# Self-attention on one Trainium2 core: the inputs' rounding moved behind a maximum of scores, the variances of the heads placed behind it, and the keys' part of the rounded inputs written first

## The chip, the cores and the metric

The kernel runs on one core of one Trainium2 chip. A core has a matrix engine (TensorE, PE in the profile, with PEld for its weight loads), a vector engine (VectorE, DVE), a scalar engine (ScalarE, ACT), a general engine (GpSimd, POOL) and an engine that only issues transfers (SyncE, SP). Each runs its own instructions strictly in order and waits on semaphores for the others. The metric is the device time of one execution in microseconds; the kernel before took 1504.7 us (median of 3 runs, 1503.29 to 1509.96).

## What is computed

The input x is 16 sequences of 128 tokens of width 256. Four blocks follow each other, each added to x: a gated attention with keys and values from x itself ("self", 16 heads in 8 groups of width 128) and from a context ("cross", 16 more heads), a feed-forward block, a causal attention with 32 small heads, and a mixture of 8 experts. The change touches the first:

```python
ln_out = _ln(hidden_states, ln_w, ln_b)
q = _ln(_fp8_linear_pertensor(ln_out, wq, wq_scale, q_in_scale).reshape(...), qln_w, qln_b)
k = _ln(_fp8_linear_pertensor(ln_out, wk, ...), kln_w, kln_b)      # each head normalised
v = _fp8_linear_pertensor(ln_out, wv, ...)
core = _gqa(q, k, v)                                               # softmax attention
qx = _ln(_fp8_linear_pertensor(ln_out, wqx, ..., qx_in_scale), ...) # queries of the cross part
...
catq = _div_clamp_fp8(cat, proj_smooth)                            # both parts, rounded
return einsum(catq, wproj) * (proj_in_scale * proj_w_scale)
```

`_fp8_linear_pertensor` divides its input by a scale per channel, clamps it to 448, rounds it to bfloat16 and then to an 8-bit float, and multiplies it by the weights. So one layer-normed x is rounded four times, for q, k, v and qx.

## The kernel before

**Units and steps.** A unit is one sequence's self or cross attention: units 0 to 15 are self, 16 to 31 cross. A unit has 16 heads in four chunks of four heads, and a loop over n (L692) makes one step per chunk: step n holds the scores of chunk n, and, shifted by fixed numbers of steps, everything else. `do(n, lag, name)` calls a stage for the chunk `lag` steps back (ahead where it is negative), `once(n, step, name)` calls a stage once per unit, at the unit's first step plus `step`. So the steps of one unit run mixed with the projections of the next and the preparation of the one after it.

**What sets the order.** The program is written in the order of these calls. A scheduler then orders each engine's instructions by its own estimate of what is ready, with the written order as priority, and puts in the semaphores; what the engines run is therefore near the written order but not equal to it. `stay_after(ins, other)` (L102) tells the scheduler that one instruction must stand behind another of the same engine, without a semaphore.

**A self unit's preparation.** `prep_norm`, `prep_tr` and `prep_scale` make the normalised x, transposed and divided by the four scales: one tile in_y of 128x1024 (four kinds of 2x128 columns, in the order q, k, v, qx), scaled on GpSimd (L387). `prep_round` (L397) rounds it with the helper `e4m3` (L219): four instructions on VectorE (L225 clamp, L226 exponent, L230, L231), each needing the one before, and a subtraction on GpSimd (L237) that `prep_last` issues one step later. It writes xs (q, k and v, 128x768) and xx (qx, 128x256); xx also goes to DRAM by the SyncE queue (L409), for the cross unit of the same sequence. The same helper, with the same lines, rounds the attention's output (`quant`, tile cat_y, 128x1024, twice a unit).

**Projections and heads.** `project` multiplies xs by the weights (L431; keys first, then queries, then values, two blocks of 512 columns a step), `evict` copies the result from PSUM on ScalarE (L443 raw for keys and queries, L440 vt for values), `bn` takes each head's statistics on VectorE (L452). `rstd` (L454) makes the 24 heads' variances of a unit (L459 q_dif, L460, L461, L464 q_var) and their inverse roots (`rsqrt0`: L308 and L309 on ScalarE, then L310 to L312 on VectorE, the last writing q_r). `mult` scales raw by q_r on GpSimd (L475), `heads` transposes it on TensorE (L486) and copies it on ScalarE into kT and qT (L495).

**Attention.** `scores` (L504), `top` (L512, the negated maximum on VectorE), `exp` (L520, four instructions on ScalarE with their sums), `recip` (L528) and `divide` (L532, GpSimd), `probs` (L540 transposes, L542 copy), `values` (L550), `smooth` (L561, VectorE, writes cat_y), `quant`, `quant_last` (L237, GpSimd, writes cat), `output` (L591).

**Where the change works.** In the third of every four steps (n = 4u + 2), the step in which the unit's third chunk has its scores, `prep_last` of the unit after next, and `rstd` of the next unit, fall together. In the kernel before, `prep_round` closes the step before that one (`once(n, -7, "prep_round")`, L735), and in the step itself the calls are: scores, probs, top, exp, a projection, `prep_last` (L710), values, smooth, bn, `rstd` (L715), then mult and heads.

Of the kernel before, what the change touches and what calls it, by code (L numbers as in the profile page):

```python
# [35 lines left out]
def flamingo_kernel(  # L36
# [182 lines left out]
    def e4m3(dsts, y, pool):  # L219


        n = y.shape[1]
        e = pool.tile([P, n], BF16, tag="e8_e", name="e8_e")
        t = pool.tile([P, n], BF16, tag="e8_t", name="e8_t")
        nc.vector.tensor_scalar(y, y, FP8_MAX, -FP8_MAX, ALU.min, ALU.max)  # L225
        nc.vector.tensor_scalar(  # L226
            e.bitcast(U16), y.bitcast(U16), 0x7F80, None, ALU.bitwise_and
        )

        nc.vector.tensor_scalar(e, e, 2.0**-6, 24.0, ALU.max, ALU.mult)  # L230
        nc.vector.tensor_tensor(t, y, e, ALU.add)  # L231

        def last(other=None):
            at = 0
            for dst in dsts:
                part = slice(at, at + dst.shape[1])
                ins = nc.gpsimd.tensor_tensor(dst, t[:, part], e[:, part], ALU.subtract)  # L237
                if other is not None:
                    stay_after(ins, other)
                at += dst.shape[1]  # L240

        return last
# [11 lines left out]
    with (  # L254
# [59 lines left out]

        norms = {}
# [19 lines left out]
        class Unit:  # L335
# [61 lines left out]
            def prep_round(self):  # L397
                if self.cross:
                    return
                xs = ap.tile([P, 6 * P], F32R, tag="xs", name="xs")  # L400
                xx = ap.tile([P, KD * P], F32R, tag="xx", name="xx")
                self.last = e4m3([xs, xx], self.y.rearrange("p i t -> p (i t)"), ap)
                self.xs, self.xx = xs, xx

            def prep_last(self):
                if self.cross:
                    return
                self.last()
                nc.sync.dma_start(out=xqx[self.b], in_=self.xx.bitcast(F32))  # L409
                lhs = [  # L410
                    [self.xs[:, (2 * kind + k) * P : (2 * kind + k + 1) * P] for k in range(KD)]
                    for kind in range(3)
                ]
                self.q_lhs, self.k_lhs, self.v_lhs = lhs[K_Q], lhs[K_K], lhs[K_V]
# [39 lines left out]
            def rstd(self):  # L454
# [4 lines left out]
                nc.vector.tensor_tensor(dif, st[:, :, 1], st[:, :, 4], ALU.subtract)  # L459
# [4 lines left out]
                nc.vector.scalar_tensor_tensor(var, var, 1.0 / P, dif, ALU.mult, ALU.add)  # L464
# [45 lines left out]
            def top(self, c):  # L510
                mx = small.tile([P, 4], F32, tag="mx", name="mx")
                nc.vector.tensor_reduce(mx, self.sc[c], AX.X, ALU.max, negate=True)  # L512
                self.mx = mx
# [42 lines left out]
            def smooth(self, c):  # L556
# [4 lines left out]
                nc.vector.tensor_tensor(  # L561
                    self.cy[:, 4 * (c % 2) : 4 * (c % 2) + 4, :], pv,
                    r_sm[:, h0 : h0 + 4, None].to_broadcast([P, 4, P]), ALU.mult,
                )

            def quant(self, c):
                if c % 2 == 0:
                    return
                cat = ap.tile([P, 8, P], F32R, tag="cat", name="cat")
                self.clast = e4m3(  # L570
                    [cat.rearrange("p h s -> p (h s)")],
                    self.cy.rearrange("p h s -> p (h s)"), ap,
                )
                self.cat[c // 2] = cat
# [117 lines left out]
        for n in range(first, last + 1):  # L692
# [12 lines left out]
            do(n, 0, "top")  # L705
            do(n, 0, "exp")
            if ab[0]:
                ab[0][0].project(ab[0][1])
                ab[0][0].evict(ab[0][1])
            once(n, -6, "prep_last")  # L710
            do(n, 3, "values")
            do(n, 3, "smooth")
            if ab[0]:
                ab[0][0].bn(ab[0][1])
            once(n, -2, "rstd")  # L715
# [19 lines left out]
            once(n, -7, "prep_round")  # L735
# [600 lines left out]
```

## Time and profile before

| what | value |
|---|---|
| median of 3 runs | 1504.7 us (1503.29 to 1509.96) |
| the profiled execution | 1506.21 us |
| its span, first to last instruction | 1504.5 us |
| mean granted TensorE clock | 0.974 |
| busy: PE / DVE / ACT / POOL | 1379.0 / 1014.0 / 811.2 / 677.6 us |
| L459 q_dif, 32 times | 188 to 1278 ns, median 202 ns |
| L237 xs 128x768 / xx 128x256 | median 1654 / 674 ns |
| L475 raw 128x512, 192 times | median 1042 ns |

How to read it: each engine's busy time is a share of the span; instructions of one engine follow each other, so that an engine which is idle waits for something another engine has yet to do. A row of the table of waits names the waiting instruction, the one that released it, the total idle time in us, how often, and the longest. In the timeline a line is one instruction or several equal ones in a row, with its start and its length in us, and in brackets how long its engine had been idle before it and what ended that. The self part runs from about 25 to 457 us of the span, the cross part to about 930 us; the rest is the three other blocks.

### The profile page before, as it was taken

To read this page: it belongs to the slowest core of one execution; us is meant where nothing else is said; L and a number is where in the kernel's file an instruction comes from. 1 tells how busy PE (TensorE), PEld (TensorE's weight loads), DVE (VectorE), ACT (ScalarE), POOL (GpSimd) and SP (SyncE) were. 2 spreads that over 40 slices of the span, in tenths; PEclk is the share of its full clock that TensorE was granted. 3 is DMA by queue.
4 is the path that set the end of the run, shared out by engine and by line. 5 is a ranking of instruction groups with operands and counts; after the bars stand their busy time and mean duration, and the time that the engine had idled before them with its cause. 6 is when DMAs were issued, how large, how long until landed. Compare 5 with 4: busy or idle time off the path is not lost. (4 is left out here: it accounts for less than half of the span.)

```text
span 1504.5 us, 24887 instructions
## 1 busy us (share of the span) xinstructions
PE 1379.0 (92%) x8644; PEld 1004.9 (67%) x8644; DVE 1014.0 (67%) x2656; ACT 811.2 (54%) x2437; POOL 677.6 (45%) x586
## 2 busy tenths in 40 slices
PE   2789899899988999999999997999999999996998
PEld 1578687787766677777777765555555666654887
DVE  7968778787787777687776765453478888882100
ACT  3766666666555666666666652164355555542121
POOL 4567666767676555656555564121021312111111
PEclk9799999999998999999999998899999999996999
DMA  4301001000023100000000001600120100012652
GB/s 133 113 16 37 20 22 41 22 23 20 22 72 92 47 22 19 15 18 15 12 21 12 15 4 31 207 8 14 52 87 9 54 9 36 9 40 73 200 189 68
DMA packets 63933, 72.18 MB, mean 48 GB/s; under 512 B 12731, under 2 KB 50043, under 8 KB 63808
## 3 DMA queue, kind: packets, MB, share of 16 engines
q1 hardware_dynamic: 50304, 46.89, 10.4%
q10 hardware_dynamic: 11456, 17.63, 3.7%
q0 software_dynamic: 2048, 6.07, 1.1%
q8 instruction: 69, 1.13, 0.3%
q14 instruction: 56, 0.46, 0.1%
HBM read 52.95 MB, written 17.86 MB: 47 GB/s over the span
## 5 line engine op out<-in xcount | busy, mean ns | idle before, releaser
L532 POOL TENSOR_TENSOR e<-e,sums 128x512 f32<-128x512 f32 x128 | 141.0, 1102 | 239.4 <-DVE sums L528 102.6
L475 POOL TENSOR_TENSOR raw<-raw,q_r 128x512 f32<-128x512 f32 x192 | 212.0, 1130 | 22.9 <-DVE q_r L312 21.5
L452 DVE BATCH_NORM_STATS2 q_st<-raw 128x6 f32<-128x128 f32 x768 | 174.1, 278 | 63.9 <-ACT raw L443 63.1
L520 ACT ACTIVATE e<-ps_sc,mx 128x128 f32<-128x128 f32 x512 | 181.5, 369 | 63.9 <-DVE mx L512 58.4
L1089 ACT ACTIVATE e<-ps_sc,mx 128x128 f32<-128x128 f32 x512 | 139.3, 383 | 112.7 <-DVE mx L1080 109.9
L591 PE MATMUL ps_acc<-wp,cat 128*128 128x512 f32 x512 | 160.5, 436 | 14.1 <-POOL cat L237 13.4
L504 PE MATMUL ps_sc<-kT,qT 128*128 128x128 f32 x1024 | 140.4, 280 | 24.4 <-ACT qT L495 24.4
L504 PEld LDWEIGHTS ps_sc<-kT,qT 128*128 128x128 f32 x1024 | 132.0, 193 | 44.5 <-ACT qT L495 37.0
L542 ACT COPY eT<-ps_tr 128x512 f32<-128x512 f32 x128 | 75.4, 589 | 157.3 <-PE ps_tr L540 157.3
L237 POOL TENSOR_TENSOR cat<-e_t,e_e 128x1024 fp32r<-128x1024 bf16 x64 | 136.8, 2138 | 43.9 <-DVE e_t L231 43.2
L550 PE MATMUL ps_pv<-eT,vt 128*128 128x256 f32 x512 | 133.9, 383 | 1.0 <-DVE cat_y L561 1.0
L591 PEld LDWEIGHTS ps_acc<-wp,cat 128*128 128x128 f32 x512 | 95.0, 192 | 54.0 <-POOL cat L237 20.4
L443 ACT COPY raw<-ps_mm 128x512 f32<-128x512 f32 x192 | 113.9, 594 | 30.5 <-PE ps_mm L431 27.3
L486 PE MATMUL ps_tr<-ident,raw 128*128 128x128 f32 x768 | 114.6, 275 | 13.0 <-POOL raw L475 11.1
L486 PEld LDWEIGHTS ps_tr<-ident,raw 128*128 128x128 f32 x768 | 91.0, 141 | 46.7 <-POOL raw L475 19.7
L561 DVE TENSOR_TENSOR cat_y<-ps_pv,r_sm 128x512 bf16<-128x512 f32 x128 | 87.0, 680 | 49.6 <-PE ps_pv L550 49.2
L550 PEld LDWEIGHTS ps_pv<-eT,vt 128*128 128x128 f32 x512 | 97.4, 192 | 31.5 <-issue 10.8
L512 DVE TENSOR_REDUCE mx<-ps_sc 128x4 f32<-128x512 f32 x128 | 87.2, 681 | 36.3 <-PE ps_sc L504 35.7
L495 ACT ACTIVATE qT<-ps_tr,hv 128x512 f32<-128x512 f32 x128 | 101.3, 791 | 18.9 <-PE ps_tr L486 16.7
L520 ACT ACTIVATION_READ_ACCUMULATOR e<-ps_sc,mx 128x1 f32 x512 | 105.4, 206 | 0.0
L1100 PEld LDWEIGHTS ps_tr<-ident,e 128*128 128x128 f32 x512 | 57.6, 140 | 58.1 <-ACT e L1089 21.7
L1045 POOL TENSOR_TENSOR kb<-kT,hmask 128x512 f32<-128x512 f32 x32 | 33.4, 1065 | 124.3 <-PE ps_sc L1073 119.2
(222 smaller groups left out, 2771.4 us busy)
## 6 DMA issues: line engine op xcount, KB each, us to landing
w1t<-in_w ACTq DMA_DIRECT2D x8, 1024.0 KB
w2t<-in_w ACTq DMA_DIRECT2D x8, 1024.0 KB
disp<-empty SPq DMA_DIRECT2D x16, 257.0 KB
xe<-disp SPq DMA_DIRECT2D x8, 514.0 KB
ctx<-in_ctxT SPq DMA_DIRECT2D x32, 128.0 KB
stage<-in_wprojT SPq DMA_DIRECT2D x16, 256.0 KB
xg<-in_x SPq DMA_DIRECT2D x4, 512.0 KB
xb<-in_x SPq DMA_DIRECT2D x16, 128.0 KB
```

The costliest lines, as they stand in the source:

```text
L237: ins = nc.gpsimd.tensor_tensor(dst, t[:, part], e[:, part], ALU.subtract)
L443: nc.scalar.copy(raw.rearrange("p h d -> p (h d)"), pm)
L452: nc.vector.bn_stats(self.st[:, 4 * blk + j, :], self.raws[blk][:, j, :])
L475: ins = nc.gpsimd.tensor_tensor(src, src, self.r[:, 4 * blk : 4 * blk + 4, None].to_broadcast([P, 4, P]), ALU.mult,)
L486: nc.tensor.transpose(pt[:, j, :], src[:, j, :], ident)
L495: nc.scalar.activation(dst, pt, AF.Identity, scale=hv[:, col : col + 1], bias=hv[:, col + 1 : col + 2])
L504: nc.tensor.matmul(pscore[:, j, :], qT[:, j, :], self.kT[:, 2 * c + j // 2, :], start=True, stop=True,)
L520: nc.scalar.activation(e[:, j, :], pscore[:, j, :], AF.Exp, bias=self.mx[:, j : j + 1], accum_out=sums[:, j : j + 1],)
L532: nc.gpsimd.tensor_tensor(e, e, sums[:, :, None].to_broadcast([P, 4, P]), ALU.mult)
L550: nc.tensor.matmul(pv[:, 2 * g : 2 * g + 2, :], self.vt[:, gg * P : (gg + 1) * P], eT[:, 2 * g : 2 * g + 2, :], start=True, stop=True,)
L591: nc.tensor.matmul(self.acc, self.cat[c // 2][:, h % 8, :], wpr[self.cross, c][:, j, :, :], start=(h == 0), stop=(h == 15),)
L1089: nc.scalar.activation(e[:, i, :], s[:, i // NQ, i % NQ, :], AF.Exp, bias=mx[:, i : i + 1])
```

## The change

The rounding of the inputs moves from the end of one step into the next, behind that step's maximum and exponentials, with its first instruction bound to stand behind the maximum (L512). The variances move ahead of values, smooth and bn, with L459 bound to stand behind the rounding's last instruction on VectorE, and the smoothing of the same step bound to stand behind the last variance (L464). The rounded inputs become four tiles of 128x256, for q, k, v and qx, which GpSimd writes one by one in the order k, q, v, qx, and no longer two tiles in two instructions. No arithmetic differs.

```diff
-    def e4m3(dsts, y, pool):
+    def e4m3(dsts, y, pool, order=(0,), ahead=None):
...
-        nc.vector.tensor_scalar(y, y, FP8_MAX, -FP8_MAX, ALU.min, ALU.max)
+        ins = nc.vector.tensor_scalar(y, y, FP8_MAX, -FP8_MAX, ALU.min, ALU.max)
+        if ahead is not None:
+            stay_after(ins, ahead)
...
-        nc.vector.tensor_tensor(t, y, e, ALU.add)
+        added = nc.vector.tensor_tensor(t, y, e, ALU.add)
 
         def last(other=None):
-            at = 0
-            for dst in dsts:
-                part = slice(at, at + dst.shape[1])
+            at = [sum(d.shape[1] for d in dsts[:i]) for i in range(len(dsts))]
+            for i in order:
+                dst = dsts[i]
+                part = slice(at[i], at[i] + dst.shape[1])
                 ins = nc.gpsimd.tensor_tensor(dst, t[:, part], e[:, part], ALU.subtract)
...
-        return last
+        return last, added
...
-            def prep_round(self):
+            def prep_round(self, n):
...
-                xs = ap.tile([P, 6 * P], F32R, tag="xs", name="xs")
-                xx = ap.tile([P, KD * P], F32R, tag="xx", name="xx")
-                self.last = e4m3([xs, xx], self.y.rearrange("p i t -> p (i t)"), ap)
+                kinds = [
+                    ap.tile([P, KD * P], F32R, tag=f"x{slot}", name=f"x{slot}")
+                    for slot in ("qs", "ks", "vs", "x")
+                ]
+                self.last, rounded[n] = e4m3(
+                    kinds, self.y.rearrange("p i t -> p (i t)"), ap, (K_K, K_Q, K_V, 3), tops.get(n)
+                )
...
-            def rstd(self):
+            def rstd(self, n):
...
-                nc.vector.tensor_tensor(dif, st[:, :, 1], st[:, :, 4], ALU.subtract)
+                ins = nc.vector.tensor_tensor(dif, st[:, :, 1], st[:, :, 4], ALU.subtract)
+                if n in rounded:
+                    stay_after(ins, rounded[n])
...
-                nc.vector.scalar_tensor_tensor(var, var, 1.0 / P, dif, ALU.mult, ALU.add)
+                vars_[n] = nc.vector.scalar_tensor_tensor(
+                    var, var, 1.0 / P, dif, ALU.mult, ALU.add
+                )
...
-                nc.vector.tensor_reduce(mx, self.sc[c], AX.X, ALU.max, negate=True)
+                tops[n] = nc.vector.tensor_reduce(mx, self.sc[c], AX.X, ALU.max, negate=True)
...
-                nc.vector.tensor_tensor(
+                ins = nc.vector.tensor_tensor(
                     self.cy[:, 4 * (c % 2) : 4 * (c % 2) + 4, :], pv,
                     r_sm[:, h0 : h0 + 4, None].to_broadcast([P, 4, P]), ALU.mult,
                 )
+                if n in rounded:
+                    stay_after(ins, vars_.get(n, rounded[n]))
...
+            once(n, -6, "prep_round", n)
             once(n, -6, "prep_last")
+            once(n, -2, "rstd", n)
             do(n, 3, "values")
-            do(n, 3, "smooth")
+            do(n, 3, "smooth", n)
             if ab[0]:
                 ab[0][0].bn(ab[0][1])
-            once(n, -2, "rstd")
...
-            once(n, -7, "prep_round")
```

More of the change, by code (lines that the diff above doesn't have):

```diff
@@ L239, in last @@
                     stay_after(ins, other)
-                at += dst.shape[1]
-        return last
+        return last, added
     xqx = dram.tile([B, P, KD * P], F32, name="xqx")
@@ L313, in rsqrt0 @@
             return r
+        tops = {}
+        rounded = {}
+        vars_ = {}
         norms = {}
@@ L395, in prep_scale @@
                 self.y = y
-            def prep_round(self):
+            def prep_round(self, n):
                 if self.cross:
                     return
-                xs = ap.tile([P, 6 * P], F32R, tag="xs", name="xs")
-                xx = ap.tile([P, KD * P], F32R, tag="xx", name="xx")
-                self.last = e4m3([xs, xx], self.y.rearrange("p i t -> p (i t)"), ap)
-                self.xs, self.xx = xs, xx
+                kinds = [
[5 more added lines that the diff above has]
+                )
+                self.xs, self.xx = kinds[:3], kinds[3]
             def prep_last(self):
@@ L410, in prep_last @@
                 lhs = [
-                    [self.xs[:, (2 * kind + k) * P : (2 * kind + k + 1) * P] for k in range(KD)]
+                    [self.xs[kind][:, k * P : (k + 1) * P] for k in range(KD)]
                     for kind in range(3)
@@ L508, in scores, with top @@
                 self.sc[c] = pscore
-            def top(self, c):
+            def top(self, c, n):
                 mx = small.tile([P, 4], F32, tag="mx", name="mx")
-                nc.vector.tensor_reduce(mx, self.sc[c], AX.X, ALU.max, negate=True)
+                tops[n] = nc.vector.tensor_reduce(mx, self.sc[c], AX.X, ALU.max, negate=True)
                 self.mx = mx
@@ L554, in values, with smooth @@
                 self.pv[c] = pv
-            def smooth(self, c):
+            def smooth(self, c, n):
                 pv = self.pv.pop(c)
@@ L569, in quant @@
                 cat = ap.tile([P, 8, P], F32R, tag="cat", name="cat")
-                self.clast = e4m3(
+                self.clast, _ = e4m3(
                     [cat.rearrange("p h s -> p (h s)")],
@@ L704, in flamingo_kernel @@
             do(n, 2, "probs")
-            do(n, 0, "top")
+            do(n, 0, "top", n)
             do(n, 0, "exp")
```

## The prediction

> **What bounds the kernel now.** The page's slices say TensorE (PE) is the engine to watch: nine tenths busy nearly everywhere. The chain that ended last covers the last 15 us only, so I went to busy time by stretch. The first row is ten heads-and-attention units of the self part, the second the change to the cross part, the third the cross part:
>
> ```profile
> 120.00:392.00 272.00, 250.08 (x1474) 209.25 (x1473) 210.53 (x632) 172.86 (x545) 190.26 (x151) 1.00 0.09 27
> 392.00:510.00 118.00, 103.59 (x546) 81.15 (x544) 91.39 (x239) 70.63 (x213) 77.32 (x64) 0.94 0.19 57
> 510.00:920.00 410.00, 399.23 (x2074) 298.04 (x2072) 295.11 (x827) 264.91 (x811) 236.19 (x184) 1.00 0.06 18
> ```
>
> PE idles 21.9 us in the ten self units, 2.2 us each; that is all that can be won there. The clock is 1.00, so it explains nothing. The table of waits names the two stalls and what stands behind them:
>
> ```profile
> PE ps_sc L504 <- ACT qT L495: 24.4, 29, 2.4
> POOL raw L475 <- DVE q_r L312: 21.5, 12, 3.3
> ACT q_a L308 <- DVE q_var L464: 13.8, 15, 2.0
> PE ps_tr L486 <- POOL raw L475: 11.1, 22, 2.0
> ```
>
> The timeline of one unit shows both (start, length, engine):
>
> ```profile
> 309.15 1.05 PE L504 MATMUL ps_sc<-kT,qT 128*128 128x128 f32 x8
> ...
> 312.14 0.75 DVE L231 TENSOR_TENSOR e_t<-in_y,e_e 128x1024 bf16<-128x1024 bf16 x1
> ...
> 312.81 0.68 DVE L512 TENSOR_REDUCE mx<-ps_sc 128x4 f32<-128x512 f32 x1
> 312.97 1.65 POOL L237 TENSOR_TENSOR xs<-e_t,e_e 128x768 fp32r<-128x768 bf16 x1 [0.63 <-DVE e_t L231]
> 313.42 1.27 DVE L459 TENSOR_TENSOR q_dif<-q_st 128x24 f32<-128x24 f32 x1
> ...
> 315.94 0.22 ACT L308 ACTIVATE q_a<-q_var 128x24 f32<-128x24 f32 x1 [0.85 <-DVE q_var L464]
> 316.07 0.76 ACT L495 ACTIVATE qT<-ps_tr,hv 128x512 f32<-128x512 f32 x1
> ...
> 316.89 1.16 PE L504 MATMUL ps_sc<-kT,qT 128*128 128x128 f32 x8 [1.46 <-ACT qT L495]
> 317.00 1.37 POOL L532 TENSOR_TENSOR e<-e,sums 128x512 f32<-128x512 f32 x1 [1.75 <-DVE sums L528]
> ...
> 317.81 0.18 DVE L312 SCALAR_TENSOR_TENSOR q_r<-q_a,ps_sc 128x24 f32<-128x24 f32 x1
> ...
> 319.45 0.63 PE L486 MATMUL ps_tr<-ident,raw 128*128 128x128 f32 x4
> ```
>
> Call the end of the third chunk's scores T = 310.20. The maximum that needs them runs 2.6 us later, behind the inputs' rounding. qT, ready to be copied at 312.9, stands on ScalarE behind q_a, which waits for the variances: PE loses 1.46 us before the last chunk's scores (stall A). Then the keys' transposes wait for the first scaled raw, at T+9.16 (stall B); they start at T+9.25. Everything after that runs in PE's order with no stall but a fixed 0.34 us for the second raw. So **the period of a unit is set by when the first raw is scaled**, and stall A is merely time taken out of the wait for it. The table of distances between q_dif starts agrees: 26.5 us where raw ends at T+9.16 (six units), 27.4 to 27.6 where it ends at T+10.08 (four units, call them caught: there 461 is blocked as well), 27.8 at T+10.65 (the two with the next batches' statistics in between).
>
> **The change part by part.** In the order that the changed program was built with, one step of VectorE reads: maximum; 225, 461, 226, 230, 231 on the inputs; 459; reciprocal 528; 460; 464; 561; then 225, 310, 226, 311, 230, 312, 231 (the cat rounding between the steps of the root). ScalarE reads: four exponentials, vt, qT, then q_a, vt, root. PE has the last chunk's scores two transposes and one matmul earlier. I walk it with the durations above.
>
> *Maximum first.* The bn block that ended at 312.23 now follows the eviction at 310.22 (0.87), so the maximum runs T+0.85 to T+1.53, not T+2.61 to T+3.29. Exponentials (1.61) end at T+3.24, vt at T+3.8, qT at T+4.5. PE reaches the scores at T+4.8: **stall A is gone, 1.46 us**. That frees no time by itself: scores, two transposes, four key matmuls (1.2) and values (1.0) then bring PE to the transposes at T+8.1, where it waits for raw.
>
> *Rounding later.* Four dependent instructions after the maximum, starts 0.45 apart as at 315.40 to 316.77, the last 0.68 long: e_t ends at T+3.5, where it ended at T+2.69. 0.8 us lost on the path to raw.
>
> *Keys' part first.* Three 128x256 parts and xx instead of 128x768 and xx: 4 x 0.675 against 1.65 + 0.675, 0.37 us more of GpSimd per unit, 32 instructions in all. The keys' matmuls can start 1.0 us sooner after e_t, but PE is not waiting for them in a steady unit (wk starts 0.3 us after xs and behind other work): worth nothing there. In the first unit, where PE waits 10.8 us for xs, the part is ready 1.4 us sooner after e_t, but two more instructions stand ahead of e_t (0.74 + 0.40): about -0.3 us. The xqx store follows xx about 1.2 us later on SP; nothing stands behind it until the next ctx load at 323.65, and its reader is 16 units on.
>
> *Variances behind the rounding, in the middle of GpSimd's four writes.* This decides. Where q_dif overlaps xs it takes 1.27 us, and 0.20 in every cross unit, where nothing overlaps. The same shows where GpSimd has instructions queued without a gap:
>
> ```profile
> 706.29 6.00 POOL L475 TENSOR_TENSOR raw<-raw,q_r 128x512 f32<-128x512 f32 x5
> 706.62 1.15 DVE L226 TENSOR_SCALAR e_e<-cat_y 128x1024 uint16<-128x1024 uint16 x1
> 707.80 1.15 DVE L230 TENSOR_SCALAR e_e<-e_e 128x1024 bf16<-128x1024 bf16 x1
> 708.98 1.41 DVE L231 TENSOR_TENSOR e_t<-cat_y,e_e 128x1024 bf16<-128x1024 bf16 x1
> ```
>
> The free lengths are 0.43, 0.43 and 0.67: each gets in at the next boundary of GpSimd's row, one per instruction, and the row is lengthened (6.00, not 5 x 1.04). The Trainium skill, page "SBUF — State Buffer", section "Who interferes with whom", says that the one which issues first holds the shared pair for its whole instruction and the other is blocked. It speaks against this change: 460 and 464 (two SBUF inputs each) and the cat rounding now meet four writes and a divide in a row. It does not say who wins when GpSimd's next one is already queued. Taken as order of issue, VectorE would wait out all five (the slower rival below); by the row it waits out one at a time, and I take the row.
>
> From e_t's end E = T+3.5: 459 slips in before the first write (it starts in e_t's tail); 460 ends with that write at E+0.8; 464 with the second at E+1.45 (before: T+5.71, now T+4.95). q_a, vt 0.6, root: est at E+2.3. 561 ends at E+2.05. 225 waits out a write, to E+2.5 or 2.95; 226 the next, to E+3.2 or the divide, E+4.15; 230 follows, and 312 ends at E+4.5 to 4.7. 231 (0.67) then holds raw back some 0.4: raw runs from there to E+6.0 to 6.2. I take E+6.15: **T+9.65 against T+9.16**. Of the 1.46 us won, nothing reaches the end of an ordinary unit: it gets 0.5 us longer. The caught units, whose extra work this order has cleared out or spread, come to the same T+9.65: 0.4 us shorter. In the statistics units the roots finish before 230, and e_t is 0.2 later: raw at T+9.3, 1.4 shorter. Unit 2, at T+10.84, gains 1.2.
>
> *Sum.* 6 x (+0.48) + 4 x (-0.43) + 2 x (-1.37) - 1.2 - 0.3 = -3.1 us. The smoothing behind q_var ends at T+5.55 where it ended at T+5.08; its pv buffer is wanted at T+7.2, its cat not before T+11: free, and if the margin of 1.6 went, one for one. The units beyond 16 keep their order. The change to the cross part (units 14 and 15, PE idle 8.3 and 3.4 us) is reordered by the scheduler on all engines: a GpSimd divide comes before a 2.1 us cat, scores move before an output; I bound it by -4 and +4 and take 0. The profiled execution took 1506.2 (span 1504.5 and 1.7 around it); the median is 1504.7. 1506.2 - 3.1 = 1503.1, so about 1501.5 for the median.
>
> **The rivals.**
> *The blocking hardly bites* (0.25). Then GpSimd's row alone sets raw: E + 0.08 + 2.72 + 1.04 + 1.04 = T+8.4; ordinary units gain 0.8, caught ones 1.7, statistics units 2.2, unit 2 2.4: 18.4 us, 1486; half of it 1495. For it: 460 took 0.17 beside the end of xx, and small operands may fit in a gap together. Against: 461 took 0.71 right behind 459 in the caught units.
> *GpSimd's queued write wins* (0.20): 460 waits for all four (E+2.8), 464 for the divide (E+3.85), root and cat rounding follow, raw ends near E+7.5 = T+11. Ordinary units lose 1.85, caught ones 0.9, statistics units 0.4: about +16, 1521. It decides from T+10.1 on, where the sum over the units passes +3. Against it: the 1.15 rows.
> *The step into the cross part decides* (0.07): it wins back 8 us of its 11.7 us of idle time, 1493 (0.02), or a late output or weight costs 12 us, 1513 (0.04); between them nothing is seen (0.01). For it: all engines' order differs there. Against: the weights' loads, which set that stretch, stand where they stood but for a few neighbours.
> *Nothing moves* is inside my case: -3 us is 0.2%.
>
> **How the numbers follow.** My case (0.48): 1501.5, its own range 1495 to 1509 (0.25 us per unit either way over 13 units, and the 4 us). A measurement of this kernel, with runs 1503 to 1510, tells about 0.5%, 7.5 us, from no change. Chances: faster 0.25 + 0.02 = 0.27, same 0.48 + 0.01 = 0.49, slower 0.20 + 0.04 = 0.24. The range, 1488 to 1519, leaves the far end of each rival out.
>
> **What would show it.** After: qT's wait before scores (24.4) falls to about 9, while raw's wait before transposes rises to some 1.2 us per self unit; self units all near 26.9, none at 27.6; 460 and 464 at 0.6 in place of q_dif's 1.27; q_r at E+4.6. Wrong if 460, 464 and 225 show free lengths (faster), or if any exceeds 1.5 us (slower), or if PE idles elsewhere than at L486.

## The result, and the profile after

| | before | after |
|---|---|---|
| median of six runs each, us | 1505.6 (1503.3 to 1510.0) | 1517.2 (1515.9 to 1518.7) |
| ratio to before, 95% interval | | 1.0079 (1.0064 to 1.0093) |
| profiled execution: its time, its span | 1506.2, 1504.5 | 1517.8, 1516.1 |

The changed kernel is 0.8% slower, where 0.2% faster was forecast. The two profiled spans differ by 11.6 us. Cut at T, the end of the third chunk's scores in each unit, they compare as follows (units are counted from 1, and each runs from its T to the next):

| stretch (units as the prediction counts them) | before, us | after, us | difference | predicted |
|---|---|---|---|---|
| up to unit 2 | 91.7 | 91.6 | -0.1 | -0.3 |
| unit 2 | 28.2 | 30.3 | +2.1 | -1.2 |
| six ordinary units (3, 6, 7, 10, 11, 12) | 159.1 | 165.5 | +6.4 | +2.9 |
| three caught units (5, 9, 13) | 82.2 | 84.4 | +2.2 | -1.3 |
| two units with statistics (4, 8) | 55.9 | 58.0 | +2.0 | -2.7 |
| units 14 and 15, the step into the cross part | 70.4 | 67.9 | -2.4 | -0.4, 4 either way |
| cross units, to T of unit 31 | 400.2 | 399.4 | -0.8 | 0 |
| all that follows | 616.9 | 619.0 | +2.1 | 0 |

The chains of single instructions went nearly as the prediction walked them. Here is a unit of after at full clock in the timeline, unit 13, with T = 402.73; it was a caught one in before, and in after it is like an ordinary one to 0.01 us (start, length, engine; in brackets the idle time before and what ended it):

```profile
405.52 0.69 DVE L233 TENSOR_TENSOR e_t<-in_y,e_e 128x1024 bf16<-128x1024 bf16 x1
...
406.13 0.20 DVE L468 TENSOR_TENSOR q_dif<-q_st 128x24 f32<-128x24 f32 x1
...
406.29 0.68 POOL L240 TENSOR_TENSOR xks<-e_t,e_e 128x256 fp32r<-128x256 bf16 x1 [2.57 <-DVE e_t L233]
406.36 0.65 DVE L471 SCALAR_TENSOR_TENSOR q_dif<-q_dif 128x24 f32<-128x24 f32 x1
...
407.04 0.60 DVE L475 SCALAR_TENSOR_TENSOR q_var<-q_var,q_dif 128x24 f32<-128x24 f32 x1
...
409.18 1.15 DVE L228 TENSOR_SCALAR e_e<-cat_y 128x1024 uint16<-128x1024 uint16 x1
409.38 1.03 PE L563 MATMUL ps_pv<-eT,vt 128*128 128x256 f32 x4
...
410.70 0.17 DVE L314 SCALAR_TENSOR_TENSOR q_r<-q_a,ps_sc 128x24 f32<-128x24 f32 x1
...
410.95 3.45 POOL L488 TENSOR_TENSOR raw<-raw,q_r 128x512 f32<-128x512 f32 x3 [0.91 <-DVE q_r L314]
...
412.46 0.66 PE L499 MATMUL ps_tr<-ident,raw 128*128 128x128 f32 x4 [2.05 <-POOL raw L488]
413.46 0.66 PE L499 MATMUL ps_tr<-ident,raw 128*128 128x128 f32 x4 [0.34 <-POOL raw L488]
```

e_t ends at T+3.48 (T+3.5 was forecast), 460 and 464 of the old line numbers (L471, L475) take 0.65 and 0.60 us, q_r ends at E+4.66, the first raw at T+9.68 and the transposes start at T+9.73: within 0.1 us of the walk. Stall A is gone, and the table of waits shows what took its place. These are the waits of PE between T of unit 3 and T of unit 14, of before and then of after (us in total, times, longest):

```profile
PE ps_sc L504 <- ACT qT L495: 16.8, 11, 1.7
PE ps_tr L486 <- POOL raw L475: 7.4, 16, 1.1
```

```profile
PE ps_tr L499 <- POOL raw L488: 27.2, 20, 2.3
PE ps_acc L606 <- POOL cat L240: 1.7, 2, 0.9
```

Waiting went from 24.2 us to 28.9, but these eleven units grew by 10.6. The rest is not waiting. The busy time of the engines by stretch, over the same units of before and after, shows it in the column of the clock and in that of PE's busy time (the columns are the stretch, its length, then busy time and instructions of PE, PEld, DVE, ACT and POOL, the granted clock of PE, and the transfers):

```profile
119.83:417.07 297.24, 272.79 (x1609) 228.18 (x1607) 229.56 (x684) 189.27 (x599) 207.95 (x165) 1.00 0.09 26
```

```profile
121.88:429.72 307.84, 278.87 (x1608) 233.37 (x1607) 236.74 (x682) 191.33 (x599) 214.71 (x188) 0.97 0.08 26
```

PE did the same matmuls in 6.1 us more. Taken unit by unit, five of the eleven ran at a clock of 0.94, the others at 1.00. Here are units 3, 7, 8, 9 and 13:

```profile
121.88:150.17 28.29, 25.90 (x148) 21.82 (x147) 20.99 (x60) 17.47 (x55) 19.48 (x17) 0.94 0.07 21
235.79:262.78 26.99, 24.60 (x148) 20.77 (x147) 21.00 (x60) 17.26 (x55) 19.48 (x17) 1.00 0.08 24
262.78:291.90 29.12, 25.08 (x148) 20.62 (x147) 22.50 (x68) 17.48 (x56) 19.65 (x17) 1.00 0.13 39
291.90:320.62 28.72, 26.29 (x148) 21.76 (x147) 22.70 (x64) 17.62 (x56) 19.48 (x17) 0.94 0.07 21
402.73:429.72 26.99, 24.60 (x148) 20.75 (x147) 20.66 (x59) 17.26 (x55) 19.49 (x18) 1.00 0.08 23
```

The trace's record of the clock has only two values, 1.0 and 0.5, and changes only on a grid of 3.413 us. Cut along this grid, the fourth of these rows, unit 9, holds a stretch in which PE is busy for 0.96 of 3.40 us, because most of the wait for raw lies in it; the next stretch runs at half clock, and the one after at full clock again:

```profile
299.50:302.90 3.40, 0.96 (x7) 0.65 (x7) 3.20 (x11) 1.48 (x9) 2.73 (x3) 1.00 0.00 0
302.90:306.30 3.40, 3.40 (x13) 2.58 (x12) 0.49 (x3) 2.14 (x5) 3.40 (x3) 0.50 0.00 0
306.30:309.70 3.40, 3.40 (x25) 3.06 (x25) 2.20 (x7) 1.14 (x4) 3.40 (x4) 1.00 0.23 61
```

In the half stretch four key matmuls took 665 ns each on average; in unit 13, at full clock, they took 416 (busy us, mean ns, idle before):

```profile
L440 PE MATMUL ps_mm<-wk,xks 128*128 128x512 f32 x4 | 2.1, 665 | 0.0
L440 PE MATMUL ps_mm<-wk,xks 128*128 128x512 f32 x4 | 1.2, 416 | 0.0
```

In before, the emptiest stretch of the steady units had PE busy for 1.71 of 3.40 us, and full clock followed:

```profile
286.80:290.20 3.40, 1.71 (x13) 1.33 (x12) 3.33 (x10) 2.83 (x10) 1.47 (x3) 1.00 0.11 39
290.20:293.60 3.40, 2.89 (x16) 2.02 (x15) 2.79 (x6) 1.45 (x8) 2.25 (x3) 1.00 0.00 0
```

So the theory for the experiments: a wait of PE that comes in one piece can empty a stretch of the grid, and then costs its own length and 1.1 to 1.7 us of half clock more; before had nearly as much waiting, but in two pieces some 3 us apart (1.46 and 0.34 us in an ordinary unit, where after has 2.05 and, 0.7 us later, 0.34). Such a half stretch lies in units 2, 3, 5, 6, 9 and 11: 3.4 us in the ordinary and 3.3 in the caught ones (each unit's length over that of its like at full clock, 27.0) and 1.4 in unit 2 (over the 28.9 us that it takes at full clock in e6 below), together 8.1 of the 11.6 us. The rival is that these units are slow by their own work and the clock only goes with it. The second open point is the units with statistics.

### The profile page after: what moved, and what is told of

Its sections match the earlier page's. It is cut to its first block, busy times and chain, and to the rows that moved or that the text cites. A ratio compares the mean times of both kernels' runs of the same rounds, so it can differ in the third digit from the quotient of the medians.

```text
span 1516.1 us, 24913 instructions
## 1 busy us (share of the span) xinstructions
PE 1387.4 (92%) x8644; PEld 1013.3 (67%) x8644; DVE 1025.5 (68%) x2656; ACT 812.7 (54%) x2437; POOL 684.8 (45%) x618
## 5 line engine op out<-in xcount | busy, mean ns | idle before, releaser
L488 POOL TENSOR_TENSOR raw<-raw,q_r 128x512 f32<-128x512 f32 x192 | 217.6, 1159 | 17.1 <-DVE q_r L314 16.0
L461 DVE BATCH_NORM_STATS2 q_st<-raw 128x6 f32<-128x128 f32 x768 | 174.3, 278 | 68.8 <-ACT raw L452 68.1
L499 PE MATMUL ps_tr<-ident,raw 128*128 128x128 f32 x768 | 120.9, 286 | 35.5 <-POOL raw L488 33.5
L499 PEld LDWEIGHTS ps_tr<-ident,raw 128*128 128x128 f32 x768 | 95.7, 146 | 72.8 <-POOL raw L488 44.9
```

The source lines that it names most:

```text
L461: nc.vector.bn_stats(self.st[:, 4 * blk + j, :], self.raws[blk][:, j, :])
L488: ins = nc.gpsimd.tensor_tensor(src, src, self.r[:, 4 * blk : 4 * blk + 4, None].to_broadcast([P, 4, P]), ALU.mult,)
L499: nc.tensor.transpose(pt[:, j, :], src[:, j, :], ident)
```

## The experiments

All ratios are to the kernel before on the same chip, with a 95% interval. "Units 3 to 13" is the time from T of unit 3 to T of unit 14; "half" counts the half-clock stretches in it. These two and the last column come from one profiled execution each; those of e3 and e4 were the second fastest and the fastest of twenty, 4.8 and 3.4 us under their medians, so most of their executions may have had more half clock than the table shows.

| | ratio | units 3 to 13, us | half | first raw ends, ordinary unit |
|---|---|---|---|---|
| before | 1 | 297.2 | 0 | T+9.16 |
| after | 1.0079 (1.0064 to 1.0093) | 307.8 | 5 | T+9.68 |
| after, again (e9) | 1.0050 (1.0027 to 1.0072) | 307.7 | 5 | T+9.68 |
| wait filled, 8 (e1) | 0.9998 (0.9985 to 1.0011) | 301.7 | 1 | T+9.69 |
| wait filled, 12 (e10) | 1.0042 (1.0030 to 1.0053) | 302.3 | 1 | T+9.68 |
| four pieces alone (e2) | 0.9968 (0.9955 to 0.9982) | 296.1 | 0 | T+9.19 |
| after, undivided (e3) | 1.0039 (1.0027 to 1.0051) | 303.8 | 3 | T+9.68 |
| after, no variances' part (e4) | 1.0021 (1.0010 to 1.0033) | 300.7 | 2 | T+9.84 |
| maximum first alone (e5) | 0.9978 (0.9968 to 0.9987) | 295.9 | 0 | T+9.56 |
| after, keys ahead (e6) | 1.0002 (0.9988 to 1.0017) | 301.0 | 0 | T+9.68 |
| before, keys ahead (e7) | 0.9960 (0.9945 to 0.9975) | 297.2 | 0 | T+9.17 |
| e4, keys ahead (e8) | 0.9971 (0.9955 to 0.9988) | 300.1 | 3 | T+9.84 |
| after, statistics behind (e13) | 1.0036 (1.0025 to 1.0048) | 305.7 | 6 | T+9.69 |
| after, longer row (e14) | 1.0096 (1.0060 to 1.0131) | 307.6 | 4 | T+10.03 |
| after, late writes (e11) | 0.9917 (0.9897 to 0.9937) | 291.4 | 2 | T+8.71 |
| e4, late writes (e12) | 0.9895 (0.9875 to 0.9916) | 285.0 | 0 | T+8.58 |
| e12, keys ahead (e15) | 0.9861 (0.9828 to 0.9894) | 284.8 | 0 | T+8.57 |

### The clock: PE's wait filled

```diff
                 pt = ps_tr([P, 4, P])
+                if blk == 0 and not self.cross:
+                    for j in range(8):
+                        nc.tensor.transpose(pt[:, j % 4, :], ident, ident)
                 for j in range(4):
```

> The changed kernel, with eight transposes of the identity added on TensorE (PE) right behind the values' matmuls of the unit's last step, into the buffer that the keys' transposes overwrite; results and all other work are the same. They take about 8 x 0.16 = 1.3 us of the 2.05 us for which PE waits there for the first scaled raw, so nothing on the path to raw moves. Theory (the wait in one piece leaves a stretch of 3.41 us in which PE is busy for less than 0.44, and the granted clock then is 0.5 for the next 3.41 us): no stretch of the self units falls under 0.44, the granted clock is 1.00 in the third to fourteenth unit, all of them without statistics take 27.0 us, and the 8.2 us of longer PE work are gone: about 1509. Rival (PE's instructions are longer because they meet other engines' accesses, or the trace's periods wander by themselves): the same number of units at 28 us and more, 1517, or 1518 with the extra work.

Nothing on the path to raw moved (T+9.69), and PE got more to do. Yet the units fell to 27.04 us, all but the two with statistics, and the clock is 1.00 in all but unit 8. Rows by unit, from unit 3 on (the fourth to sixth are units 6 to 8):

```profile
120.57:147.62 27.05, 25.52 (x156) 21.42 (x155) 21.01 (x60) 17.30 (x55) 19.49 (x17) 1.00 0.07 22
147.62:176.52 28.90, 25.89 (x156) 21.43 (x155) 22.49 (x68) 17.40 (x56) 19.67 (x18) 1.00 0.13 41
176.52:203.56 27.04, 25.51 (x156) 21.42 (x155) 22.20 (x64) 17.36 (x56) 19.51 (x17) 1.00 0.07 22
203.56:230.61 27.05, 25.52 (x156) 21.42 (x155) 21.01 (x60) 17.29 (x55) 19.48 (x17) 1.00 0.08 23
230.61:257.63 27.02, 25.50 (x157) 21.43 (x155) 21.00 (x60) 17.28 (x55) 19.48 (x17) 1.00 0.07 23
257.63:287.09 29.46, 27.21 (x157) 22.53 (x155) 22.50 (x68) 17.63 (x56) 19.68 (x18) 0.94 0.13 40
```

That decides it for the units: the same instructions, with idle time turned into useless work, are 6.1 us faster over eleven units (307.8 to 301.7). The rival, units slow by themselves, is out. Nor is it one execution alone: the mean clock of the whole span was 0.963 to 0.968 in the six executions of the changed kernel and 0.973 to 0.983 in the twelve of this one, though on another chip.

> The changed kernel itself once more, on the chip and beside the runs of the three kernels that follow. Theory (where the stretches at half clock fall depends on where the unit's wait meets the 3.41 us grid, and that differs from execution to execution): ratio to the kernel before 1.004 to 1.009, with another set of self units at half clock than in the first profile, while the first raw ends at T+9.7 in every ordinary unit again. Rival (certain units are slow by their own work): the same units, 3, 5, 6, 7, 9 and 11, are longer than 27.0 us.

The ratio is in the range, the reason given for it failed: the same units were at half clock. The grid fits this too, though no run decides it: against the program's first instruction it stood at 2.53 us in the first profile and at 2.23 in this one, while over the seventeen profiles of this study it stood anywhere from 0.07 to 3.29. These two happened to start alike; the executions that were only timed, 1512.7 to 1519.8, need not have.

```diff
-                    for j in range(8):
+                    for j in range(12):
```

> The changed kernel with twelve transposes of the identity, not eight, in PE's wait ahead of the keys' transposes: 12 x 0.16 = 1.9 of its 2.05 us, results the same. Theory: no stretch of the self units, those with statistics included, is followed by half clock, the ordinary units take 27.0 to 27.1 us; ratio to the kernel before 0.999 to 1.003, and 0.3 to 0.8 per cent under the changed kernel of the same call. Rival (the first filled kernel came near the time before by the chip it ran on): no more than 0.2 per cent under the changed kernel of the same call.

In the units it came as expected: all ordinary and caught ones 27.0 us at full clock, 5.3 us less over units 3 to 13 than the changed kernel on the same chip (e9). Unit 8, with statistics, still had a half stretch. The mean clock of the whole span rose from 0.968 to 0.977 by the medians. In the total, though, 3.1 us were left by the medians, 0.2%, and no difference by the intervals, so as to the total the rival's figure is the nearer one. The profile shows where part of it was lost: in the step into the cross part PE's order differs, with the twelve transposes in it, and it took 70.9 us against 68.1. So filling is shown to bring the clock back in these units; the whole kernel came back to the time before in e1 (0.9998), but not here (1.0042).

### The three parts one by one

e2 changes `e4m3`, `prep_round` and the slices that `prep_last` takes from its tiles in the kernel before as the change does, and nothing else:

```diff
...
-                xs = ap.tile([P, 6 * P], F32R, tag="xs", name="xs")
-                xx = ap.tile([P, KD * P], F32R, tag="xx", name="xx")
-                self.last = e4m3([xs, xx], self.y.rearrange("p i t -> p (i t)"), ap)
+                kinds = [
...
+                self.last = e4m3(
+                    kinds, self.y.rearrange("p i t -> p (i t)"), ap, (K_K, K_Q, K_V, 3)
+                )
...
```

e3 takes this part out of the changed kernel:

```diff
...
-                    kinds, self.y.rearrange("p i t -> p (i t)"), ap, (K_K, K_Q, K_V, 3), tops.get(n)
+                    [xs, xx], self.y.rearrange("p i t -> p (i t)"), ap, (0, 1), tops.get(n)
...
```

e4 puts the variances of the changed kernel back and drops their two ties:

```diff
             once(n, -6, "prep_last")
-            once(n, -2, "rstd", n)
...
                 ab[0][0].bn(ab[0][1])
+            once(n, -2, "rstd", n)
...
-                if n in rounded:
-                    stay_after(ins, rounded[n])
...
-                if n in rounded:
-                    stay_after(ins, vars_.get(n, rounded[n]))
```

e5 is both of the last two edits together, so the maximum's part alone.

> The kernel before, with the inputs' part written in four pieces of 128x256, the keys' first; maximum, rounding and variances stand where they stood. Theory: GpSimd's row gets 0.37 us longer, in the six ordinary units the first raw ends at T+9.5 instead of T+9.16 (+0.35 us each, some 2 us in all), q_dif waits for a write of 0.68 instead of 1.65 us; no stretch at half clock in the self units, since PE's wait stays in two pieces: 1506 to 1509. Rival (the four pieces are the harm, by blocking VectorE at every boundary): the units grow as in the changed kernel, 1513 or more.

Faster, by 0.3%, which neither theory nor rival had. The ordinary units lost nothing: GpSimd's writes are 0.37 us longer, but it stood idle for 1.75 us behind them, until the sums for its divide were there (the bracket at L532 in the prediction's timeline), and the longer writes only fill that; raw starts at T+8.16 for T+8.12. The caught units won 0.46 each, T+10.08 to T+9.62, because what VectorE waits out is now 0.68 us long and not 1.65. The part that the prediction called worth nothing in a steady unit was the good one. Not all of it is placed: of the 4.5 us by the medians the profile shows 1.4 in the three caught units and 1.8 in the step into the cross part.

> The changed kernel with the inputs' part written as before, 128x768 and then 128x256; rounding behind the maximum and variances behind the rounding as changed. Theory (the order on VectorE sets the wait, not the pieces): the first raw still ends at T+9.5 to T+9.9, PE's wait is one piece of about 2 us, and stretches at half clock are there as in the changed kernel: 1512 to 1518. Rival (the pieces are the harm): raw ends at or before T+9.16 and the time is that of the kernel before, 1505.

The first raw ends at T+9.68 with two writes as with four. So the wait comes from the order on VectorE, as this theory said, and stretches at half clock follow it without the four writes too.

> The changed kernel without the variances' part: rounding behind the maximum, keys' part first, but the heads' variances stand again behind the fresh statistics, so that VectorE mixes them with the rounding and ends e_t later (about T+5.3, not T+3.5). Theory: GpSimd's four writes and the divide then start later, the first raw ends at T+10.2 or later, PE waits 2.6 us in one piece, and more units than in the changed kernel get a stretch at half clock: 1520 to 1530. Rival (the variances amid the writes are the harm): raw ends before T+9.7 and the time falls under 1512.

The theory failed, and the rival had the time right (1511.9 us) but not its reason: e_t ended at T+4.47 and raw at T+9.84, later than with the ties, all units alike, those with statistics included, and two stretches were at half clock. By the ratios the time is 0.3 to 0.6% lower than with the ties.

> The kernel before with the rounding behind the maximum alone: inputs' part written 128x768 and then 128x256, variances behind the fresh statistics. Against the kernel without the variances' part it undoes the four pieces. Theory: VectorE ends e_t near T+4.5 and the variances before it, GpSimd's row (1.65, 0.68, divide 1.04) sets the first raw, which ends at T+9.4 to T+9.6; the keys' matmuls wait some 0.5 us for the undivided write, so PE's wait comes in two pieces of 0.5 and 1.5 us; at most two self units have a stretch at half clock: ratio to the kernel before 0.998 to 1.003. Rival (taking stall A away is a loss by itself, whatever stands behind): the wait is one piece of 2 us or more and the ratio is 1.005 or above.

As expected, with the ratio a hair under the range, and the plainest sight of the mechanism. Here PE waits 22.2 us in these units, hardly less than in before (24.2), and in pieces, first 0.5 us for the undivided write, 2 us later 1.2 and 0.34 for raw; no stretch of these units at half clock, and the kernel is 0.2% faster than before. The keys' part written first takes the first piece away (e4), and what PE then waits for raw, 27.4 us, is in one piece again. PE's waits in units 3 to 13 of e5, then of e4:

```profile
PE ps_tr L495 <- POOL raw L484: 17.0, 22, 1.2
PE ps_mm L438 <- POOL xs L240: 5.2, 11, 0.5
```

```profile
PE ps_tr L497 <- POOL raw L486: 27.4, 20, 2.2
```

### What sets a unit: useful work in the wait

The same edit is made in the changed kernel (e6), in the kernel before (e7) and in e4 (e8):

```diff
+            if ab[1] and (n + 1) % 4 == 0:
+                ab[1][0].project(ab[1][1])
             for blk in range(2):
                 once(n, -2, "mult", blk)
                 once(n, -1, "heads", blk)
...
             if ab[1]:
-                ab[1][0].project(ab[1][1])
+                if (n + 1) % 4:
+                    ab[1][0].project(ab[1][1])
                 ab[1][0].evict(ab[1][1])
```

> The changed kernel, with the next unit's second block of key matmuls (1.18 us) issued on PE ahead of the keys' transposes, not behind them: it does in PE's wait what was done after it. Theory (PE's wait for the first scaled raw is the price of a unit, and the stretch at half clock comes from its length): first raw still ends at T+9.7, the wait shrinks from 2.05 to 0.9 us, nine units without statistics take 25.8 us, none at half clock; 11 x 1.18 = 13 us less than at full clock before this edit: ratio to the kernel before 0.990 to 0.995. Rival (something behind the wait, an eviction or the root on ScalarE, becomes the bound): units stay at 26.5 us or more, ratio 0.998 to 1.004.

The rival was right. None of these units is at half clock, which takes 6.8 us off units 3 to 13, but an ordinary unit still takes 27.0 us. What PE did in the wait it lost again at the output's matmuls, which now wait for cat (units 3 to 13 of e6):

```profile
PE ps_tr L499 <- POOL raw L488: 17.5, 22, 1.4
PE ps_acc L606 <- POOL cat L240: 10.3, 11, 1.9
```

So a unit at full clock is set by GpSimd's row from the first raw on: three raws, then the cat write of 2.1 us, then the output's matmuls. Without the move PE comes to the same matmuls by its own order at T+13.82, 0.05 us after cat; that the two came out at the same time was chance.

> The kernel before, with the same move of the second block of key matmuls ahead of the keys' transposes. Theory: here stall A (1.46 us) lies ahead of these matmuls and is not filled; of stall B an ordinary unit wins nothing to 0.34 us, a caught one 0.84, one with statistics about 1.2: 2 to 8 us in all, ratio 0.995 to 0.999, so the move is worth more to the changed kernel than to the one before. Rival (the move is worth the same in both, since a unit's price is the sum of its waits): ratio 0.992 or below.

The ratio is in the range, for another reason: units 3 to 13 did not move at all (297.2), for cat again. Of the 5.6 us by the medians, the profile shows 5.0 in the cross units, where the same line moves key matmuls too: 395.2 us against 400.2.

> The changed kernel without the variances' part (maximum first and four pieces stay), with the second block of key matmuls ahead of the keys' transposes. Theory: the first raw ends at T+9.85 in all units, those with statistics too; PE's wait shrinks from 2.2 to 1.0 us, all self units take 26.0 us, none at half clock: ratio 0.989 to 0.994, as good as or better than with the variances' part. Rival (the variances' part is what makes the rest pay): ratio 0.997 or above.

The ratio just falls in the rival's range, but its reason is out: on the same chip the kernel with the variances' part and keys ahead (e6) is 0.3% slower than this one. The theory failed too: units of 27.14, cat late by 0.86, three of them at half clock although PE's wait lay in three pieces (1.27, 0.34, 0.86 us) and it was busy for 0.52 to 0.53 of the stretch ahead. Dividing a wait is no safeguard by itself. Most of the 0.5% over e4 is again the cross units' (395.1 us against 400.1).

### The units with statistics

In after, VectorE stands ahead of e_t in units 4 and 8 and waits for a load, the next four batches of x, that it used to reach later. VectorE's wait in units 3 to 13:

```profile
DVE st L331 <- DMA xg<-in_x: 1.9, 2, 1.0
```

e_t ends at T+4.64 and T+4.82, not at the T+3.7 forecast. The edit splits load and statistics and holds the latter behind the variances:

```diff
-                    stats(m // 4)
+                    xgs[m // 4] = fetch(m // 4)
...
             once(n, -7, "prep_scale")
+            for m in range(0, B, 4):
+                if n == 4 * m - 10:
+                    stats(m // 4, xgs[m // 4], vars_.get(n))
...
```

> The changed kernel with the next four batches' statistics held behind the variances on VectorE, so that they no longer stand ahead of e_t waiting 1.03 us for their load. Theory (that wait is what the units with statistics lose): e_t ends at T+3.5 in all units, and the two such units of the steady part take 27.0 to 27.6 us, not 28.9 and 29.1; third to fourteenth unit 3 to 4 us less at equal clock, unit 2 1 to 2 us less; ratio 1.000 to 1.005. Rival (their extra instructions cost it, wherever they stand): e_t at T+3.5 but raw still at T+10.1 or later, those units over 28.4 us.

e_t ends at T+3.5 in all units, and unit 8 takes 27.0 us at full clock (first row), like any other. Unit 4 takes 28.35 with a half stretch in it. The cause is shown. The second row is units 3 to 13: they fell by 2 us only, since now six of them are at half clock, with as much waiting for raw as in after (26.9 us for 27.2); the grid met them otherwise.

```profile
261.37:288.39 27.02, 24.62 (x149) 20.76 (x147) 20.66 (x59) 17.30 (x55) 19.53 (x18) 1.00 0.14 42
121.95:427.61 305.66, 278.79 (x1608) 234.45 (x1607) 233.79 (x682) 190.79 (x599) 214.25 (x188) 0.97 0.08 26
```

### The row lengthened and shortened

e14 writes the residual's part twice:

```diff
-                    kinds, self.y.rearrange("p i t -> p (i t)"), ap, (K_K, K_Q, K_V, 3), tops.get(n)
+                    kinds, self.y.rearrange("p i t -> p (i t)"), ap, (K_K, K_Q, K_V, 3, 3), tops.get(n)
```

> The changed kernel with the residual's part of the inputs written twice, the same values, so that GpSimd's row ahead of the first raw is 0.68 us longer; results the same. Theory: the first raw ends at T+10.4, PE's wait is 2.7 us in one piece, ordinary units take 27.7 us at full clock, and with the longer wait at least eight of the eleven units have a stretch at half clock (1.1 to 1.7 us each), where the changed kernel has five: 10 to 16 us over the changed kernel, ratio 1.012 to 1.018. Rival (the length of the wait doesn't decide on the clock): about five units at half clock, ratio 1.010 or below.

Both numbers of the theory failed; the rival's held. Raw ended only 0.35 us later: GpSimd had waited 0.91 us for q_r (the bracket in the timeline above), half of the new write went into that wait (0.45 us are left), and q_r came 0.35 us later. And a longer wait, 2.39 us for 2.05, gave no more half stretches, four for five. An ordinary unit now takes 27.34 us, which is 8.01 steps of the grid (27.34 / 3.413): from unit 9 on, the wait falls on the same place of the grid each time, astride a boundary, with PE busy for 0.44 to 0.49 of the emptier side, and the clock stays full:

```profile
321.76:349.10 27.34, 24.60 (x148) 20.76 (x147) 21.35 (x60) 17.26 (x55) 20.29 (x18) 1.00 0.07 23
349.10:376.44 27.34, 24.60 (x148) 20.75 (x147) 21.36 (x60) 17.27 (x55) 20.30 (x18) 1.00 0.07 23
```

The length of the wait is not enough to tell; its place on the grid decides with it. At 27.0 us, 7.91 steps, the wait wanders by 0.31 us from unit to unit and now and then most of it falls into one stretch.

e11 (from the changed kernel), e12 (from e4) and e15 (e12 with the keys ahead) put the two writes that nobody waits for behind cat:

```diff
-                self.last()
-                nc.sync.dma_start(out=xqx[self.b], in_=self.xx.bitcast(F32))
+                self.last(None, (K_K, K_Q))
...
+            def prep_rest(self):
+                if self.cross:
+                    return
+                self.last(cats[-1] if cats else None, (K_V, 3))
+                nc.sync.dma_start(out=xqx[self.b], in_=self.xx.bitcast(F32))
...
-                    self.clast(units[b].scaled if b < NU else None)
+                    cats.append(self.clast(units[b].scaled if b < NU else None))
...
+            once(n, -5, "prep_rest")
```

> The changed kernel with the values' and the residual's part of the inputs (two of the four 128x256 writes) put behind the following cat write on GpSimd; their readers come two steps later. Theory (the unit is set by GpSimd's row: writes, divide, three raws, cat, then the output's matmuls; filling PE's wait won nothing because these then waited 0.73 us for cat): the first raw ends 1.0 to 1.5 us earlier, at T+8.2 to T+8.7, PE's wait falls under 1 us, ordinary units take 25.5 to 26.0 us, no stretch at half clock; ratio 0.991 to 0.995. Rival (the root, not GpSimd, holds raw back, or the late writes hold up the next ones): raw ends at T+9.5 or later, or units stay at 26.9 us: ratio 1.002 or above.

0.8% faster than before, 1.3 to 1.6% faster than the changed kernel. q_r, no longer held up by the third and fourth write, ends at T+7.17 for T+8.14, raw at T+8.71. A unit takes 26.03 us, a little over the range; PE's wait is 1.07 and 0.34 us, not under 1 in all, and the two units with statistics still had a half stretch each.

> The same two late writes in the changed kernel without the variances' part. Theory: e_t ends at T+4.5 as in that kernel, two writes to T+5.85, the divide to T+7; the factors are there at about T+7.3, the first raw ends at T+8.3 to T+8.6 in all units, those with statistics too; all eleven take 25.6 to 26.0 us: ratio 0.989 to 0.993, at or under the one with the variances' part. Rival as for that one: 0.998 or above.

All eleven units take 25.9 us, none at half clock. Without the variances' part the same two late writes are worth more, since the units with statistics lose nothing.

> The kernel with late writes and without the variances' part, and with the second block of key matmuls ahead of the keys' transposes as well. Theory (GpSimd's row of raws and cat still sets the unit): PE's wait of 1.3 us ahead of the transposes falls to 0.35, but a wait for cat of 0.4 to 0.9 us stands in its place; units 25.7 to 25.9 us, ratio 0.988 to 0.991. Rival (PE's order behind raw sets it): units 24.9 to 25.2 us, ratio 0.982 to 0.985.

Units of 25.9 us still, with 0.34 us of wait for raw and 0.86 for cat: the row of raws and cat is what is left. The whole is 1486.8 us (median), 1.4% faster than before and under the range, since the keys ahead gave 4.4 us in the cross units (396.0 for 400.4 in e12), which the expectation had not counted. PE's waits in units 3 to 13, and these units as a whole:

```profile
PE ps_acc L609 <- POOL cat L241: 9.5, 11, 0.9
PE ps_tr L504 <- POOL raw L493: 3.8, 11, 0.3
```

```profile
119.73:404.48 284.75, 271.38 (x1608) 228.40 (x1607) 218.43 (x682) 187.29 (x598) 215.46 (x188) 1.00 0.09 28
```

## Why the prediction was wrong

**Right, by its own steps.** *Maximum first*: stall A went; qT's wait ahead of scores fell from 24.4 to 6.5 us (about 9 forecast). *Rounding later*: e_t at T+3.48. *Variances in the middle of the four writes*: each of VectorE's instructions waits out one write and no more; 0.65, 0.60, 1.15 us, q_r at E+4.66. The two rivals about this blocking are out: in ordinary units raw ended neither at T+8.4 nor past T+10.1. At full clock the ordinary units grew by 0.5 us each and the caught ones shrank by 0.4, as summed.

**Wrong, first: "Of the 1.46 us won, nothing reaches the end of an ordinary unit: it gets 0.5 us longer."** At full clock that is what happened. But the step priced a wait at its length. Moving 1.46 us from the scores to the transposes made one wait of 2.05 us, with 0.34 us right behind it, out of two pieces, and this emptied stretches of the clock's grid: 8 us, more than the whole sum. The wait itself was under-sized as well: PE was at the transposes at T+7.7 and not at T+8.1, so 2.05 us stood where the working had 1.55 and the list of signs 1.2. And stall B was misread for before: in an ordinary unit there the first transposes start right behind the values' matmuls, without idle time of PE, and only the second raw's 0.34 us is idle time of PE. The term put at nothing is in "The clock is 1.00, so it explains nothing": it was 1.00 by a small margin, 0.50 of the emptiest stretch busy, where every one under 0.40 was followed by half clock. Filling the wait (e1, e10, e6) or having it in pieces (e5) took nearly all of the half clock out of these units, with raw where it was or 0.12 us earlier.

**Wrong, second: "In the statistics units the roots finish before 230, and e_t is 0.2 later: raw at T+9.3, 1.4 shorter."** e_t was 1.1 to 1.3 us later than in their neighbours and raw ended at T+10.1 and T+10.3, because the statistics' first instruction had come ahead of e_t and waited about 1 us for its load; PE then waited another 0.9 for cat. The two units gained 2.0 us where 2.7 were to be lost: 4.7 off. The step counted the extra instructions and not the load behind them (e13).

**Wrong, third: "Unit 2, at T+10.84, gains 1.2."** Its maximum runs at T+2.7, behind eight fresh statistics, so that e_t, which is now tied behind it, ends at T+5.38 for T+3.97; raw at T+11.56. With its half stretch that makes 3.3 us off.

**The claim behind all three**, that "the period of a unit is set by when the first raw is scaled", holds well at full clock: apart from the two units with statistics in the changed kernel, a unit is 17.3 us longer than the time at which raw ends, in before (26.48 and 9.16), after (26.99 and 9.68), e14 (27.34 and 10.03) and e12 (25.90 and 8.58). The reason given, PE's order behind raw, holds only in part: raw also counts because cat comes behind it in GpSimd's row (e6, e15), so a unit gains from an earlier raw but not from a better order on PE. And the keys' part first, counted as 0.3 us in the prologue, is worth 0.3% alone, some 5 us (e2): in part because it shortens what VectorE waits out in the caught units, which the sum gave to the order alone.

The step into the cross part (-2.4) stayed in its bounds. The last row of the first table, +2.1 us, lies almost wholly in blocks that the change does not touch. Half clock does not explain it (46.9 us of it there before, 45.8 after), and its cause stays open.

## What to carry to other kernels

Before taking a stall out, ask where its time will come back: two waits of PE some 3 us apart can be harmless where one of about the same sum is not, since half clock can follow it. Look at the emptiest 3.4 us of PE around the place and at what would lie in it after the change. What counts is how much of the wait lies in one such stretch, not the number of its pieces (e8). And when PE's wait is filled and nothing is won, follow the engine that it waited for to its next product: that row is the bound, and the cheapest gain is to move out of it whatever nobody awaits.

## What the runs showed of the hardware

**The clock's threshold.** The Trainium skill, page "TensorE: Matmul & The Clock Gate", section "What's actually happening", says that the clock halves after at least one idle window of about 3.4 us, on a grid that runs free of the kernel. The grid and the two values agree with the record here. The idle window does not: a stretch ahead of half clock need not be idle. In all profiles of this study together, of the stretches at full clock between 80 and 930 us, where the self and cross parts lie, every one with PE busy for less than 0.40 was followed by half clock (69 of 69); of those from 0.40 to 0.45, 19 of 30; from 0.45 to 0.50, 8 of 27; from 0.50 to 0.55, 5 of 44; of the fuller ones none. Why stretches of equal share differ stays open.

**Busy in the trace is not what the clock goes by.** In the later blocks, up to 1500 us, half clock also followed 32 stretches with PE busy for more than 0.55. Four of them, in e6 and e7, were busy throughout, but for 1.63 of their 3.41 us with fourteen matmuls of eight columns each. Transposes do count: the filling of e1 was of nothing else, and the clock stayed full. What else counts, and how much, was not tried.

**A longer wait need not cost more of the clock.** e14's units, 0.35 us longer than the changed kernel's, met the grid in step with it and had four half stretches for five in these profiles; the kernel as a whole was not faster for it.
